# Edge convolution on Trainium2: three products by differences of rows for two blocks of rows, and norms in pairs of images

## The chip, the cores and the metric

The kernel runs on one core of one Trainium2 chip. The metric is the device time of one execution in microseconds (us). PE is the core's TensorE, DVE its VectorE, ACT its ScalarE, POOL its GpSimd; SP is the sync engine, which here only issues transfers. Everything is float32.

## The reference

The network works on 16 images of 32 channels and 128 x 128 pixels through four layers, each `x = x + layer(group_norm(x))`. The change touches the start of the last layer, which is cut here to what matters:

```python
def _norm(x):                     # over all channels and pixels of one image
    return (x - mean(x)) / std(x)

def get_operator(x):              # five edge maps, 3x3 taps, reflecting pad
    b1 = _norm(0.5*corr(x, SOBEL_X) + 0.5*corr(x, SOBEL_Y))
    b2 = _norm(0.5*corr(x, SCHARR_X) + 0.5*corr(x, SCHARR_Y))
    b3 = _norm(corr(x, LAPLACE3))
    b4 = _norm(0.5*corr(x, ROBERTS_X) + 0.5*corr(x, ROBERTS_Y))
    b5 = _norm(0.5*corr(x, PREWITT_X) + 0.5*corr(x, PREWITT_Y))
    return concatenate([b1, b2, b3, b4, b5], axis=1)      # 160 channels

y = maxpool2(conv3x3(get_operator(x), conv1_w, conv1_b))  # 160 -> 32 channels
# six more convolutions, two poolings and three deconvolutions follow,
# and the layer returns x * y
```

Edge operator and first convolution are linear, so the kernel joins them for each image into one 5 x 5 convolution of 32 to 32 channels, whose weights depend on the image through the five means and standard deviations.

## The kernel before

`network` (line 2072) runs layer0, layer1_offsets, layer1_scan, layer1_sample, layer2, layer3_edges and layer3_net one after the other. Only `layer3_edges` (line 1436) is concerned. It makes the joint convolution and the horizontal half of its pooling, and writes the result to `p1` in HBM; `layer3_net` takes the rest of the pooling and of the layer from there.

The input of an image lies in tile `t` (`image`, line 1708): 128 partitions are 4 image rows x 32 channels, and the free dimension has 33 such groups of four rows, each of 132 pixels. Group i of `t` holds the image rows 4i-2 to 4i+1. The four output rows 4r to 4r+3 therefore need groups r and r+1, and the weights stand in two matrices, `W[:, 0]` for group r and `W[:, 1]` for group r+1, for each of five horizontal taps. The next taps (5 to 10) of `W` hold weights for the corrections of the left and right border. `conv` (line 1788) makes four groups of output rows at once into one PSUM bank: 5 taps x 2 matrices, ten matmuls of 128 x 128 by 512 (line 1794). The first and last step of an image add matmuls for the upper and lower border (lines 1802 and 1807). VectorE adds the border columns' corrections in PSUM (line 1812) and takes the maximum of horizontal neighbours (line 1813). Every fourth step ScalarE's queue issues four transfers to `p1` (line 1859). An image has eight steps.

Before an image can be convolved its five means and variances must be known. `stats` (line 1560) is a generator: an image is two strips, and a strip loads tile `a`, makes the five edge maps on VectorE (lines 1586 to 1614), and ScalarE sums each map and its square in two passes (`keep`, lines 1577 to 1583, passes at 1579 and 1581). It yields six times in a strip. Maps live in five rotating buffers with the tag `f`; the row sums `R`, `H` (in R's buffer) and `B2` have a buffer each. `weights` (line 1630) turns the statistics of a batch of images, at most four, into `Eb`, `Bb` and `vec`: two small matmuls for means and variances, then twenty for the weights (lines 1668 and 1672) in PSUM tiles `pw` copied by ScalarE, and a last few (lines 1687 to 1701), with `rm` copied by VectorE (line 1691). `expand` (line 1733) spreads one image's part of that over the partitions by 14 transfers on SP's queue. `corrections` (line 1751) makes the border columns of an image by small matmuls (lines 1759 to 1779) and a ScalarE copy (line 1785).

The loop at line 1838 goes over the images. It loads the next image, makes the corrections of this one and its eight steps, and after each step advances the statistics generator by two (line 1853) if they are not far enough ahead. After the fifth step it makes the weights of the next batch, if the next image opens one. The batches are images 0; 1; 2 and 3; 4 and 5; 6 and 7; 8 to 11; 12 to 15 (`cut_at`, line 1822). PSUM has four banks for `ps`, two for the tag `pg` and one for `pc`.

The order of instructions inside an engine is not written out by hand in this function. The framework lays each engine's queue in advance, by the order of the program as a priority and a cost model's idea of when operands are ready; other layers fix the order with `in_order` (line 48), this one doesn't. [...]

Of the kernel before, what the change touches and what calls it, by code (L numbers as in the profile page):

```python
# [10 lines left out]
F32 = mybir.dt.float32  # L11
AF = mybir.ActivationFunctionType
ALU = mybir.AluOpType
AX = mybir.AxisListType
PSUM = bass.MemoryType.PSUM
DRAM = bass.MemoryType.DRAM

P = 128
B, T, HW = 16, 32, 128
# [1416 lines left out]
def layer3_edges(tc, w, x3, p1, sb3, b3, groups=range(NG)):  # L1436
# [4 lines left out]


    nc = tc.nc
    V = nc.vector
    NB = 11 * 5 * T
    NX = NB + 2 * 3 * 11 * T
    with ExitStack() as ctx:
        cp = ctx.enter_context(tc.tile_pool(name="ec", bufs=1))
        psum = ctx.enter_context(tc.tile_pool(name="ep", bufs=4, space=PSUM))
        psg = ctx.enter_context(tc.tile_pool(name="epg", bufs=2, space=PSUM))  # L1450
        psc = ctx.enter_context(tc.tile_pool(name="epc", bufs=1, space=PSUM))
        bcol = load(nc, cp, w["c1_b"], "c1_b")
# [3 lines left out]
        ones = cp.tile([P, P], F32, name="ones", tag="ones")  # L1456
# [103 lines left out]
        def stats(images, mv):  # L1560
# [4 lines left out]
            for n, (b, h) in enumerate(strips):  # L1565
# [7 lines left out]
                def made(tag, rows=16, cols=HW):  # L1573
                    bufs = 5 if tag == "f" else 1
                    return fp.tile([P, rows, cols], F32, name=tag, tag=tag, bufs=bufs)

# [31 lines left out]
                keep(4, f5)  # L1608
                H = made("R", 18, HW + 1)[:, :, 0:HW]
                V.tensor_add(H, a[:, :, 2 : HW + 2], a[:, :, 0:HW])  # L1610
# [140 lines left out]
        def corrections(j, t, W, Wb, vec):  # L1751

            e = slice(32 * j, 32 * j + 1)
            pc = psc.tile([P, 2, 32], F32, name="pc", tag="pc")
            first = True
# [31 lines left out]

        def conv(n, j, t, W, Wb, vec, cs, pl):

            ps = psum.tile([P, 4, HW], F32, name="ps", tag="ps")  # L1790
            low = 1 if n == 7 else 0
            for i in range(10):
                k, d = divmod(i, 5)
                nc.tensor.matmul(  # L1794
                    ps, W[:, k, d], t[:, 4 * n + k : 4 * n + k + 4, d : d + HW],
                    start=(i == 0), stop=(i == 9 and n not in (0, 7)), skip_group_check=True,
                )
            if n in (0, 7):
                e = slice(32 * j, 32 * j + 1)
                o = ps[96 * low : 96 * low + 32, 3 * low]  # L1800
                for d in range(5):
                    nc.tensor.matmul(
                        o, Wb[:, low, d], t[:, 32 * low, d : d + HW],
                        start=False, stop=False,
                        tile_position=(0, 96 * low), skip_group_check=True,
                    )
                nc.tensor.matmul(
                    o, vec[e, low], ones[e], start=False, stop=True,
                    tile_position=(32 * j, 96 * low), skip_group_check=True,
                )  # L1810
            v = ps[:, :, 0 : HW : HW - 1]
            V.tensor_add(v, v, cs[:, :, 4 * n : 4 * n + 4].rearrange("p s r -> p r s"))
            V.tensor_reduce(
                pl[:, 4 * (n % 4) : 4 * (n % 4) + 4],
                ps.rearrange("p y (x c) -> p y x c", c=2), AX.X, ALU.max,
            )

# [3 lines left out]
        made = 0  # L1821
        cut_at = [0, 1, 2, 4, 6, *range(8, len(images), 4), len(images)]

        def advance(upto):
            nonlocal made
            while made < upto:
                next(it, None)
                made += 1

        def batch(m):  # L1830

            end = min(c for c in cut_at if c > m)
            advance(12 * end + 1)
            return weights(images[m], images[end - 1] + 1, mv)

        vec = batch(0)
        nxt = image(*divmod(images[0], 4)), *expand(0)
        for m, b in enumerate(images):
            g, j = divmod(b, 4)
            t, W, Wb = nxt  # L1840
            v = vec
            if m + 1 < len(images):
                g1, j1 = divmod(images[m + 1], 4)
                t1 = image(g1, j1)
                if m + 1 not in cut_at:
                    nxt = t1, *expand(j1)
            cs = corrections(j, t, W, Wb, v)
            for n in range(8):
                if n % 4 == 0:
                    pl = op.tile([P, 16, 64], F32, name="pl", tag="pl")  # L1850
                conv(n, j, t, W, Wb, v, cs, pl)
                if m < 6 or made < 12 * (m + 2) + 3 * n:
                    advance(min(made + 2, 12 * len(images) + 1))
                if n == 4 and m + 1 < len(images) and m + 1 in cut_at:
                    vec = batch(m + 1)
                    nxt = t1, *expand(j1)
                if n % 4 == 3:
                    for r in range(4):
                        nc.scalar.dma_start(
                            p1[g][T * j : T * j + T, r, 4 * n - 12 : 4 * n + 4],  # L1860
                            pl[32 * r : 32 * r + 32],
                        )

# [451 lines left out]
```

## Time and profile before

| quantity | value |
| --- | --- |
| median of 3 runs | 17435.32 us (17428.0 to 17453.31) |
| the profiled execution's own time | 17403.99 us |
| its span, first to last instruction | 17402.1 us |
| mean granted clock of TensorE | 0.938 |
| busy over the span: PE, DVE, ACT, POOL | 89%, 84%, 70%, 56% |
| first strip of statistics of layer3_edges starts | 14887.3 us |
| last strip of statistics ends | about 16172.9 us |
| last pooling (line 1813) ends | about 16519.2 us |
| last transfer of pooled rows lands | about 16524.6 us |

The profile is of one execution. A window's row gives the busy time of each engine, the number of its instructions in brackets, then the clock granted to TensorE (1.0 is full speed), the busy share of the DMA engines and GB/s. A group's row gives the source line, the engine, the operation, output and inputs with their shapes and the count; after the first bar the busy time in us and the mean of one in ns; after the second the engine's idle time just before these instructions and what ended most of it. A row of waits gives who waited for whom, the total in us, how often, and the longest. A row of the chain gives start and length in us. Shares of busy time over the whole span are averages over seven layers; what bounds layer3_edges is read from its own stretch.

### The profile page before, as it was taken

The page shows a single profiled execution, that of the slowest core. Times are in us where ns is not written, and L with a number is a line of the kernel's source. Part 1 is how long each engine was busy: PE and PEld are TensorE (multiplying, and loading weights), DVE is VectorE, ACT ScalarE, POOL GpSimd, SP SyncE. Part 2 cuts the span into 40 slices and gives each one's busy share as a digit, 9 for nine tenths or more (in the row PEclk, how much of TensorE's full clock was granted, in tenths as well). Part 3 has the DMA queues.
Part 4 walks back from the last instruction along what each step waited for, and adds up shares of the span by engine and source line. Part 5 has one row for each costly group of instructions (what it writes and reads, how often), then busy time and mean ns, then how long its engine had stood idle before and what let it go on. Part 6 is the DMA issues. An engine that isn't in the chain of part 4 may idle for free. (4 is left out here: it accounts for less than half of the span.)

```text
span 17402.1 us, 300113 instructions
## 1 busy us (share of the span) xinstructions
PE 15532.7 (89%) x113588; PEld 5966.0 (34%) x113588; DVE 14616.2 (84%) x14651; ACT 12173.3 (70%) x23604; POOL 9783.9 (56%) x18465
## 2 busy tenths in 40 slices
PE   8999999999999888888888888899999988699988
PEld 3333333333333222222222222255555552244433
DVE  9999999999999769999999999888888886777223
ACT  7888888888888557777777777688888882565111
POOL 9999999999999527778887788500000000000000
PEclk9999999999999989999999999898999889788988
DMA  0000000000000574445544445577777779444245
GB/s 22 12 12 12 12 12 17 12 12 12 12 16 7 84 145 160 160 161 159 162 163 156 164 164 167 160 191 196 195 195 196 199 177 222 71 84 76 57 122 176
DMA packets 1519824, 1884.48 MB, mean 108 GB/s; under 512 B 146789, under 2 KB 866717, under 8 KB 1507558
## 3 DMA queue, kind: packets, MB, share of 16 engines
q1 hardware_dynamic: 1413414, 1688.04, 37.6%
q0 software_dynamic: 26624, 93.35, 1.6%
q10 hardware_dynamic: 78336, 83.90, 1.5%
q8 instruction: 893, 14.63, 0.3%
q14 instruction: 557, 4.56, 0.1%
HBM read 1561.58 MB, written 229.64 MB: 103 GB/s over the span
## 5 line engine op out<-in xcount | busy, mean ns | idle before, releaser
L235 POOL TENSOR_SCALAR Rp<-su,nv 128x128 f32<-128x128 f32 x16384 | 5804.7, 373 | 84.7 <-PE pS L241 50.9
L224 DVE TENSOR_TENSOR Rd<-pu,nv 128x2048 f32<-128x2048 f32 x2176 | 4881.3, 2279 | 69.5 <-PE pS L241 65.6
L239 ACT ACTIVATE Ra<-su,bv 128x128 f32<-128x128 f32 x14336 | 4284.7, 388 | 530.2 <-PE pS L241 523.0
L241 PE MATMUL pS<-Rd,zw 128*32 128x512 f32 x17408 | 2903.6, 603 | 221.4 <-DVE Rd L224 220.3
L822 DVE TENSOR_TENSOR_SCAN hh<-dd,state,pd 128x512 f32<-128x512 f32 x2304 | 2824.1, 1267 | 151.6 <-PE py L856 13.5
L843 POOL TENSOR_TENSOR hh<-hh,bc 128x2048 f32<-128x2048 f32 x512 | 2319.2, 4530 | 467.0 <-DVE state L830 455.5
L241 PE MATMUL pS<-Rp,zw 128*32 128x512 f32 x8192 | 1998.6, 597 | 164.1 <-POOL Rp L235 158.3
L807 PE MATMUL pd<-du,spread 32*128 32x512 f32 x4608 | 1349.5, 660 | 570.1 <-DVE hh L822 563.0
L1228 POOL DMA_DIRECT2D x<-ob x64 | 91.5, 1430 | 3107.3 <-DVE ob L1227 2770.4
L799 ACT ACTIVATE dd<-dd,m_a 128x512 f32<-128x512 f32 x2304 | 1515.4, 714 | 336.9 <-DMA dd<-dm 329.2
L817 DVE TENSOR_TENSOR pd<-pd,bc 128x1024 f32<-128x1024 f32 x1152 | 1401.5, 1217 | 57.3 <-ACT bc L780 56.6
L241 PE MATMUL pS<-Ra,zw 128*32 128x512 f32 x7168 | 1273.3, 599 | 0.0
L1236 ACT ACTIVATE yd<-yd,nrow 128x2048 f32<-128x2048 f32 x512 | 1238.2, 2418 | 46.4 <-DMA yd<-ymap 46.4
L1116 ACT ACTIVATE ya<-pb,nrow 128x1024 f32<-128x1024 f32 x1024 | 1191.3, 1250 | 85.3 <-PE pb L1115 85.2
L1115 PE MATMUL pb<-Y,sel 32*128 32x512 f32 (+1 forms) x5120 | 1080.7, 740 | 165.9 <-ACT ya L1116 163.1
L1794 PE MATMUL ps<-t,W 128*128 128x512 f32 x2560 | 1146.6, 607 | 0.0
L241 PEld LDWEIGHTS pS<-Rd,zw 128*32 128x32 f32 x17408 | 615.2, 109 | 1236.4 <-issue 593.2
L807 PEld LDWEIGHTS pd<-du,spread 32*128 32x128 f32 x4608 | 373.3, 191 | 1608.6 <-DVE hh L822 713.3
L1120 DVE TENSOR_SCALAR yd<-yd 128x2048 f32<-128x2048 f32 x512 | 726.5, 1419 | 197.1 <-ACT yd L1236 195.8
L241 PEld LDWEIGHTS pS<-Rp,zw 128*32 128x32 f32 x8192 | 440.5, 110 | 1303.0 <-POOL Rp L235 845.0
L1120 DVE TENSOR_SCALAR ya<-ya 128x2048 f32<-128x2048 f32 x512 | 760.1, 1484 | 11.1 <-ACT ya L1116 9.9
L1127 PE MATMUL pd<-ya,xt 128*32 128x128 f32 x16384 | 690.7, 311 | 41.9 <-DVE ds L1280 30.0
(411 smaller groups left out, 23131.6 us busy)
## 6 DMA issues: line engine op xcount, KB each, us to landing
dd<-dm SPq DMA_DIRECT2D x2304, 256.0 KB
yd<-ymap SPq DMA_DIRECT2D x512, 1024.0 KB
hw<-x SPq DMA_DIRECT2D x192, 512.0 KB
dm<-dt POOLq DMA_DIRECT2D x192, 256.0 KB, 3.7
xb<-tok SPq DMA_DIRECT2D x248, 144.0 KB
w<-d SPq DMA_DIRECT2D x64, 528.1 KB
x<-in_x SPq DMA_DIRECT2D x64, 512.0 KB
x<-o SPq DMA_DIRECT2D x128, 256.0 KB
```

What stands on the lines that cost most here:

```text
L224: nc.vector.tensor_tensor(R, st["pu"].unsqueeze(1).to_broadcast([P, 4, 4, HW]), nv[:, :, i::32].rearrange("p t q -> p q t").unsqueeze(3).t ...
L235: nc.gpsimd.tensor_scalar(R[:, q, k], su[:, k], 3.4028234e38, nv[:, k, c], ALU.min, ALU.max)
L239: nc.scalar.activation(R[:, q, k], su[:, k], AF.Relu, bias=bv[:, k, c])
L241: nc.tensor.matmul(st["pS"][32 * q : 32 * q + 32], zw[:, 31 - i : 63 - i], R[:, q], start=first, stop=False, tile_position=(0, 32 * q), sk ...
L799: S.activation(dd[:, r], dd[:, r], AF.Exp, scale=acol[:, dr, d : d + 1])
L807: nc.tensor.matmul(pd[:, a], spread[e, k], st["du"][n][e], start=True, stop=True)
L817: V.tensor_mul(pd, pd, bm.unsqueeze(1).to_broadcast([P, 2, CH]))
L822: V.tensor_tensor_scan(hh[:, r, s], dd[:, r, s], pd[:, a, s], st["state"][:, 4 * i + r : 4 * i + r + 1], ALU.mult, ALU.add,)
L843: G.tensor_mul(hh, hh, st["bc"][1, n].unsqueeze(1).to_broadcast([P, 4, CH]))
L1116: S.activation(dst[:, 2 * h : 2 * h + 2], pb, AF.Abs, bias=nrow)
L1120: V.tensor_scalar(t, t, 1.0, 1.0, ALU.min, ALU.subtract)
L1236: S.activation(yd, yd, AF.Abs, bias=nrow)
```

## The change

Two neighbouring groups of output rows, r and r+1 with r even, are

    y(r)   = W0 t(r)   + W1 t(r+1)
    y(r+1) = W0 t(r+1) + W1 t(r+2)

which is four products. The changed kernel makes three:

    both   = (W0 + W1) t(r+1)
    y(r)   = both + W0 (t(r)   - t(r+1))
    y(r+1) = both + W1 (t(r+2) - t(r+1))

A step of `conv` covers eight groups of rows, and an image has four steps. A new function `prepare` makes an image's corrections, the sum of the two matrices (into the taps 5 to 9 of `W[:, 0]`, which only the corrections read) and a copy of the last group of `t`; it is called after the third step of the image before, together with `expand`. A new function `differences` makes the differences on VectorE, one half into a tile `d` with one buffer, the other in place in `t`; it is called behind the last step of the image before. ScalarE copies the product `both` to SBUF, VectorE adds it to each of the two others into a tile `y`, and corrections and maximum work on `y`. The pooled rows leave after every step of eight groups. The batches of norms become images 0; 1; and then pairs. The statistics advance by four after a step, under a changed condition. Maps, `R`, `H` and `B2` share five buffers of one size. PSUM has five banks for `ps` and three for `pg`, which takes `pc` too.

```diff
-        psum = ctx.enter_context(tc.tile_pool(name="ep", bufs=4, space=PSUM))
-        psg = ctx.enter_context(tc.tile_pool(name="epg", bufs=2, space=PSUM))
-        psc = ctx.enter_context(tc.tile_pool(name="epc", bufs=1, space=PSUM))
+        psum = ctx.enter_context(tc.tile_pool(name="ep", bufs=5, space=PSUM))
+        psg = ctx.enter_context(tc.tile_pool(name="epg", bufs=3, space=PSUM))
...
                 def made(tag, rows=16, cols=HW):
-                    bufs = 5 if tag == "f" else 1
-                    return fp.tile([P, rows, cols], F32, name=tag, tag=tag, bufs=bufs)
+                    t = fp.tile([P, 18 * (HW + 1)], F32, name=tag, tag="f", bufs=5)
+                    return t[:, 0 : rows * cols].rearrange("p (r w) -> p r w", w=cols)
...
-                H = made("R", 18, HW + 1)[:, :, 0:HW]
+                H = made("H", 18)
...
-            pc = psc.tile([P, 2, 32], F32, name="pc", tag="pc")
+            pc = psg.tile([P, 2, 32], F32, name="pc", tag="pg")
...
+        def prepare(g, j, t, W, Wb, vec):
+
+            cs = corrections(j, t, W, Wb, vec)
+            V.tensor_add(W[:, 0, 5:10], W[:, 0, 0:5], W[:, 1, 0:5])
+            end = sp.tile([P, HW + 4], F32, name="end", tag="end")
+            nc.scalar.copy(end, t[:, 32])
+            return g, j, t, W, Wb, vec, cs, end
+
+        def differences(t):
+            d = xp.tile([P, 16, HW + 4], F32, name="d", tag="d", bufs=1)
+            V.tensor_sub(d, t[:, 0:32:2], t[:, 1:33:2])
+            V.tensor_sub(t[:, 2:33:2], t[:, 2:33:2], t[:, 1:33:2])
+            return d
...
+            def product(w, x, row=None):
+                ps = psum.tile([P, 4, HW], F32, name="ps", tag="ps")
+                for dx in range(5):
                     nc.tensor.matmul(
+                        ps, w[:, dx], x[:, :, dx : dx + HW], start=(dx == 0),
+                        stop=(dx == 4 and row is None), skip_group_check=True,
                     )
...
+            both = op.tile([P, 4, HW], F32, name="both", tag="both", bufs=2)
+            nc.scalar.copy(both, product(W[:, 0, 5:10], t[:, r + 1 : r + 8 : 2]))
+            pl = op.tile([P, 8, 64], F32, name="pl", tag="pl")
+            for k in range(2):
+                if k == 0:
+                    ps = product(W[:, 0, 0:5], d[:, 4 * n : 4 * n + 4], (0, 0, t[:, 0]) if n == 0 else None)
+                else:
+                    ps = product(W[:, 1, 0:5], t[:, r + 2 : r + 9 : 2], (1, 3, end) if n == 3 else None)
+                y = op.tile([P, 4, HW], F32, name="y", tag="y", bufs=1)
+                V.tensor_add(y, ps, both)
...
-        cut_at = [0, 1, 2, 4, 6, *range(8, len(images), 4), len(images)]
+        cut_at = [0, 1, *range(2, len(images) + 1, 2)]
...
+            for n in range(4):
+                conv(n, now, d)
+                if m < 3 or made < 12 * (m + 2) + 4 * n:
+                    advance(min(made + 4, 12 * len(images) + 1))
+                if n == 2 and more:
+                    if m + 1 in cut_at:
+                        vec = batch(m + 1)
+                    nxt = prepare(g1, j1, t1, *expand(j1), vec)
+            if more:
+                d = differences(t1)
```

More of the change, by code (lines that the diff above doesn't have):

```diff
@@ L1786, in corrections @@
             return cs
[L1788 to L1796, printed above, removed]
-                )
[L1798 to L1809, printed above, removed]
-                )
[L1811 to L1816, printed above, removed]
@@ new lines, in conv @@
+        def conv(n, now, d):
+            g, j, t, W, Wb, vec, cs, end = now
+            e = slice(32 * j, 32 * j + 1)
+            r = 8 * n
+            def product(w, x, row=None):
+                ps = psum.tile([P, 4, HW], F32, name="ps", tag="ps")
+                for dx in range(5):
+                    nc.tensor.matmul(
+                        ps, w[:, dx], x[:, :, dx : dx + HW], start=(dx == 0),
+                        stop=(dx == 4 and row is None), skip_group_check=True,
+                    )
+                if row is not None:
+                    low, m, x = row
+                    o = ps[96 * low : 96 * low + 32, m]
+                    for dx in range(5):
+                        nc.tensor.matmul(
+                            o, Wb[:, low, dx], x[:, dx : dx + HW], start=False, stop=False,
+                            tile_position=(0, 96 * low), skip_group_check=True,
+                        )
+                    nc.tensor.matmul(
+                        o, vec[e, low], ones[e], start=False, stop=True,
+                        tile_position=(32 * j, 96 * low), skip_group_check=True,
+                    )
+                return ps
+            both = op.tile([P, 4, HW], F32, name="both", tag="both", bufs=2)
[8 more added lines that the diff above has]
+                V.tensor_add(y, ps, both)
+                v = y[:, :, 0 : HW : HW - 1]
+                V.tensor_add(
+                    v, v, cs[:, :, r + k : r + k + 7 : 2].rearrange("p s r -> p r s")
+                )
+                V.tensor_reduce(
+                    pl[:, k:8:2], y.rearrange("p y (x c) -> p y x c", c=2), AX.X, ALU.max
+                )
+            for k in range(4):
+                nc.scalar.dma_start(
+                    p1[g][T * j : T * j + T, k, r : r + 8], pl[32 * k : 32 * k + 32]
+                )
@@ L1836, in layer3_edges @@
         vec = batch(0)
-        nxt = image(*divmod(images[0], 4)), *expand(0)
+        g, j = divmod(images[0], 4)
+        nxt = prepare(g, j, image(g, j), *expand(j), vec)
+        d = differences(nxt[2])
         for m, b in enumerate(images):
[L1839 to L1842, printed above, removed]
+            now = nxt
+            more = m + 1 < len(images)
+            if more:
                 g1, j1 = divmod(images[m + 1], 4)
                 t1 = image(g1, j1)
[L1845 to L1862, printed above, removed]
+            for n in range(4):
[6 more added lines that the diff above has]
+                    nxt = prepare(g1, j1, t1, *expand(j1), vec)
+            if more:
+                d = differences(t1)
 def layer3_net(tc, w, x3, p1, out, sb3, b3, groups=range(NG)):
```

## The prediction

> **What bounds the kernel now.** I read the cut of the span into windows first, then the groups of the edge convolution's time by line and form, its waits, and the chain that ended last. The change touches layer3_edges alone, which runs from 14887 us (first strip of statistics) to 16518.6 us (last pooling). The windows cut its image loop, roughly, into images 0 and 1, 2 and 3, 4 and 5, 6 and 7, 8 to 11, 12 to 15.
>
> ```profile
> core 0: us, PE busy (x) PEld busy (x) DVE busy (x) ACT busy (x) POOL busy (x), PEclk, DMA share, GB/s
> 15010.00:15262.00 252.00, 230.50 (x690) 97.17 (x689) 178.53 (x152) 142.78 (x191) 2.88 (x14) 0.87 0.40 70
> 15262.00:15453.00 191.00, 188.44 (x532) 81.00 (x531) 153.17 (x126) 121.27 (x160) 3.28 (x16) 0.89 0.47 83
> 15453.00:15651.00 198.00, 191.82 (x543) 83.07 (x539) 151.33 (x119) 119.39 (x155) 3.28 (x16) 0.88 0.42 75
> 15651.00:15887.00 236.00, 194.81 (x543) 87.10 (x544) 181.11 (x143) 148.16 (x190) 3.68 (x18) 0.83 0.46 84
> 15887.00:16222.00 335.00, 334.83 (x1049) 156.19 (x1048) 194.78 (x169) 145.09 (x187) 6.16 (x30) 0.98 0.35 66
> 16222.00:16519.00 297.00, 296.24 (x900) 138.25 (x898) 27.51 (x65) 13.88 (x13) 4.33 (x31) 0.98 0.23 47
> ```
>
> PE is never idle for long, but VectorE (DVE) follows at about 150 us in each 195. Only in the last row, where the statistics are over, is PE alone. So there are two parts: up to 16172 us (last strip done) two engines are near their limit, after it one is. The chain shows the pure PE part, and that the order inside an engine is not the program's (line 1603 stands after line 1598 in the program):
>
> ```profile
> 14899.05 2.20 DVE f L1603
> 14901.25 2.20 DVE f L1598
> ...
> 16299.69 60.43 PE ps L1794 x140
> ...
> 16377.98 60.43 PE ps L1794 x140
> ```
>
> 140 passes take 60.43 us, 0.432 us each. A float32 matmul is two passes in the trace (2560 = 16 images x 8 blocks x 10 taps x 2), so an image's convolution is 160 x 0.432 = 69.1 us; from one image to the next it is 78.3 us, the other 9.2 us being border rows and corrections. The groups give the prices:
>
> ```profile
> L1794 PE MATMUL ps<-t,W 128*128 128x512 f32 x2560 | 1146.6, 607 | 0.0
> ...
> L1579 ACT ACTIVATE f<-f 128x2048 f32<-128x2048 f32 x160 | 304.6, 1904 | 300.3 <-DVE f L1588 138.9 <-DVE f L1598 110.5 <-DVE f L1607 25.9
> L1813 DVE TENSOR_REDUCE pl<-ps 128x256 f32<-128x512 f32 x128 | 88.0, 688 | 2.3
> L1586 DVE TENSOR_TENSOR R<-a 128x2322 f32<-128x2322 f32 x32 | 82.3, 2571 | 13.5 <-DMA a<-x 12.2 <-ACT a L1557 1.1
> ...
> L1603 DVE TENSOR_TENSOR f<-a 128x2048 f32<-128x2048 f32 x32 | 73.1, 2285 | 0.1
> ```
>
> and the waits from 14887 to 16172 us show where VectorE's time goes unused:
>
> ```profile
> DVE ps L1812 <- PE ps L1794: 148.4, 37, 7.7
> ...
> DVE rm L1691 <- PE pr L1687: 68.0, 4, 22.9
> ...
> DVE ps L1812 <- PE ps L1807: 43.0, 12, 9.6
> ```
>
> In that stretch of 1285 us VectorE was busy 963.5 us (same windows view, one window), so unused 321.5: 191.4 waiting for convolution products (the first and third line), 94.8 waiting at line 1691 for the norm's matmuls (68.0, and 26.8 put down to line 1672), 35 in small gaps.
>
> [...] the batch of norms from 15208 to 15241 us, after gaps of 6.4, 6.7 and 7.5 us, was granted 0.50 and took 33 us; the one from 16178 to 16203 us, without a gap, 1.00 and 25 us with some convolution among it. [...] line 1691 stood up to 22.9 us with strip work behind it. [...]
>
> **Part by part.** Products: eight groups of rows now take three products of 5 taps, 30 passes or 12.96 us, where they took 40 passes, 17.3 us. Per image 120 passes, 51.8 us, instead of 69.1; with the unchanged 9.2 us an image is 61.0 us of PE, 17.3 less, 276 us over 16 images. That is an upper bound, as most of it lies beside VectorE's work.
>
> VectorE per image: 8 adds of product and copy, PSUM and SBUF to SBUF, 512 elements: lines 283 and 266 do that shape in 0.674 and 0.679[...]; 0.69 x 8 = 5.5. The small add (0.17) and the pooling (0.69) stay, now in SBUF. Two differences of 2112 elements: [...] between lines 1603 (2.285) and 1586 (2.571): 4.7. [...] Together 11.0 us an image. This lies on the engine with least room.
>
> ScalarE per image: 4 copies of 512 from PSUM (line 189: 0.572) 2.3; one row of 132, 0.25 (line 1725: 0.25 for 33 elements) to 0.30; 8 more DMA issues at 0.31 to 0.43 on its queue, 3.4 at most. 6 us an image: I take nothing, as ScalarE is 60% busy and the rest covers it; without cover 16 x 6 = 96. The pooled rows leave in two buffers for every eight groups instead of every sixteen; the last transfer took 5.34 us and a step takes 13 or more, so nothing, or the excess if it lands late. Its new wait is different: the copy waits for a PE product, with the statistics' Square and Identity passes queued behind it, and VectorE waits for those to get its map buffers back. From zero (PE is ahead) to one product, 4.3 us, four times an image.
>
> Buffers: the maps, R, B2 and H share five buffers where there were seven. A map is done on ScalarE about 4.4 us after VectorE made it and its buffer is wanted again five tiles, some 11 us, later. So nothing, unless ScalarE is over 6 us late; then each such case costs VectorE the excess. PSUM banks 4+2+1 become 5+3: between a small gain and nothing, I take nothing.
>
> Norms: nine batches for seven, each 25 (warm) to 33 us (cold) of PE and 2.84 us of VectorE, whose wait at line 1691 averaged 94.8/6 = 15.8. Against that, no batch needs four images' statistics at once: the 236 us window, with 25 us of empty PE, goes.
>
> Moves: expanding the weights (14 SP issues, 8 x 0.63 + 6 x 0.57 = 8.5 us, behind the strip loads; two POOL memsets of 0.4) and the corrections go from the image's start to the third of four steps of the image before. The fourth step's three products (13 us) hide them; uncovered, 8.5 us and a landing would stand before the image. The weights' sum waits for the corrections and the differences stand behind the image's last steps of statistics: new waits at each image's start. With the differences made, the first product that uses them is 4.3 us away, and the second another 4.3; VectorE needs about 1.6 us of work in between, so it waits some 5 us (0, if strip work is put there, to 17 if PE is cold and each takes 8.6).
>
> The sum, as VectorE's ledger to its last strip. Busy 963.5. Added, for 13.75 images instead of 12 pooled by then: adds 110 x 0.69 = 76; 14 more poolings at 0.86 = 12; differences 14 x 4.7 = 66; weights' sums 14 x 0.82 = 11; two batches 6: together 171. Unused: 8 batches x 15.8 = 126, 14 image starts x 5 = 70, small gaps 35: 231 instead of 321, since the waits for products, 191, came from a PE that filled the whole 191 to 198 us of a pair, and now needs 122 + 33 = 155. The last strip ends at 14887 + 964 + 171 + 231 = 16253. From there the last batch took 31 us before (16172.9 to 16204), corrections and sum 6, two images 122, last pooling 2: 16414 against 16518.6. Saved 105 us. The profiled execution took 17404.0 us with a span of 17402.1, so 17299 of it; the median of the three runs is 17435.3, 31 above, and with the same saving gives 17330.
>
> **Rivals.** (a) The ledger above: 17330. (b) VectorE finds strip work for most of its waits, which the free order of the queues allows, and only batches stop it: unused 130 instead of 231, saved 206, 17230. PE's own sum allows it: from 15016, 16 x 61 + 9 x 30 = 1246 to 16262, and about 50 of early waiting for statistics, as before at 15186 to 15208. (c) The unused time stays 321 because every engine now waits for another; saved 15, 17420. For it: ScalarE's new wait and the five buffers. Against it: PE has 35 us of slack in a pair. (d) Slower: at each image start VectorE stands for cold products. Mechanism: the differences stand behind up to four steps of statistics (about 18 us); PE has only the shared product to do[...]. It decides above 5 + 105/14 = 12.5 us per start; at 17, 14 x 12 = 168 more, 63 lost, 17498. For it: PEclk already 0.83 to 0.89 where both engines work. Against it: the free order can bring the differences forward.
>
> **Numbers.** Chances: (a) 0.47, (b) 0.20, (c) 0.16, (d) 0.17. A measurement of this kernel tells 0.2%, 35 us, from no change, so from 17400 to 17470 counts as none. (a) and (b) are faster, (c) mostly within, (d) slower: 0.70, 0.13, 0.17. The range takes (a) to (c) with the bounds of the costs, 25 to 30 us on each side: 17200 to 17450, leaving out (d).
>
> **What would show it.** PE's convolution passes at 1920 with the same 0.432 us when warm; a pure image 61 us at the end; 128 adds at 0.69 and 32 differences at 2.36; last strip near 16253, last pooling near 16414; pairs of some 176 us; VectorE over 85% busy between. Wrong if pairs exceed 187 us, the average before from 15242 us, when image 2 starts, to 16362, when image 14 does, or PEclk falls below 0.8 there.

## The result, and the profile after

The changed kernel takes 17368.33 us (median of 5 runs, 17350.89 to 17383.67) beside 17443.89 us for the kernel before (5 runs, 17428.0 to 17481.99): a ratio of 0.9952, 95% interval 0.9938 to 0.9967, or 76 us saved where 105 were forecast. The profiled execution took 17350.89 us, its span is 17349.1 us, the mean granted clock 0.931. The first strip of statistics starts at 14891.0 us (before 14887.3), the last ends at 16271.8 us (forecast 16253), the last pooling at 16460.5 us (forecast 16414, before 16519.2).

In the lines of the changed kernel the products are at 1812, the copy `both` at 1831, its add at 1839, the pooling at 1844, the differences at 1799 and 1800, the sum of the matrices at 1792, the norms' matmuls at 1648, 1654, 1669, 1673 and 1688, and the copy `rm` at 1692. The windows cut the image loop, roughly, into pairs of images (us, then busy time and count of PE, PEld, DVE, ACT and POOL, then granted clock, DMA share, GB/s):

```profile
15025.00:15269.00 244.00, 182.42 (x513) 76.66 (x514) 189.33 (x163) 134.62 (x184) 3.39 (x16) 0.76 0.36 65
15269.00:15428.00 159.00, 148.91 (x463) 68.09 (x464) 145.60 (x131) 99.92 (x137) 2.99 (x14) 0.90 0.51 91
15428.00:15620.00 192.00, 164.82 (x463) 71.76 (x464) 138.69 (x127) 99.50 (x136) 3.39 (x16) 0.78 0.41 73
15620.00:15809.00 189.00, 160.92 (x479) 70.08 (x478) 158.00 (x136) 112.40 (x151) 3.39 (x16) 0.80 0.48 86
15809.00:15994.00 185.00, 161.16 (x447) 70.36 (x448) 137.77 (x127) 95.48 (x129) 3.39 (x16) 0.80 0.42 75
15994.00:16178.00 184.00, 162.58 (x494) 71.21 (x493) 145.87 (x130) 103.49 (x143) 3.39 (x16) 0.81 0.45 83
16178.00:16341.00 163.00, 159.19 (x465) 69.63 (x466) 98.16 (x110) 72.41 (x99) 3.39 (x16) 0.86 0.31 58
16341.00:16460.00 119.00, 117.80 (x346) 54.52 (x345) 31.82 (x53) 9.44 (x13) 1.49 (x19) 0.96 0.16 35
```

The last row is two images of PE alone, 119 us, at a granted clock of 0.96: the saving is there in full. From the first pooling of image 14 to the last pooling the kernel before took 141 us (16378 to 16519), the changed one 106 (16354 to 16460): 35 less, and two images at 17.3 are 34.6. All 14 images ahead of them, which have 14 x 17.3 = 242 us fewer of products, are only 24 us earlier (28 counted from the first strip). Only images 2 and 3, the row from 15269, still keep both engines over 90% busy. In the four rows from 15428 to 16178, VectorE is busy 138 to 158 us of 184 to 192, and PE, which has 122 us of images to do there at full clock, shows 161 to 165 at a granted clock of 0.78 to 0.81.

Where the rest went can be counted in the two timelines of PE: the stretches of more than 8 us in which no product runs, from the first product on, are six before, of 9 to 81 us, and add up to 243 us; in the changed kernel they are eight, of 20 to 94 us, and add up to 463. These 220 us more are about what is missing.

The timeline of PE around the end of one pair shows what such a stretch holds (start, us, engine, line and operation, in brackets PE's idle time before it and what ended it):

```profile
15546.26 4.47 PE L1812 MATMUL ps<-t,W 128*128 128x512 f32 x10
15550.66 1.28 PE L1820 MATMUL ps<-end,Wb 128*32 128x128 f32 x10
...
15557.42 0.60 PE L1648 MATMUL pm<-ms,avg 128*128 128x10 f32 x2 [5.14 <-DVE ms L1644]
15563.55 0.60 PE L1654 MATMUL pv<-ms,avg 128*128 128x10 f32 x2 [5.54 <-DVE ms L1652]
15569.20 1.86 PE L1669 MATMUL pw<-base,l 128*64 128x480 f32 x2 [5.04 <-DVE l L1664]
...
15607.37 1.46 PE L1760 MATMUL pc<-t,W 128*128 128x32 f32 x6 [4.13 <-DMA W<-Eb]
...
15619.58 2.08 PE L1812 MATMUL ps<-t,W 128*128 128x512 f32 x2 [6.92 <-DMA a<-x]
```

The batch of norms for the next two images lies behind the last product of this pair, so PE has nothing else to do. It waits three times some 5 us for VectorE, the twenty `pw` matmuls run at half clock (0.50 granted) until 15598.9, then come the transfers of the expanded weights, the corrections and the weights' sum (the profile puts the last wait down to a load of `a`; the sum ended at 15619.52, so it was the sum). From 15552.3, the last border matmul, to 15619.6 no product runs: 67 us. Two images at 61 and that gap are 189. The batches for images 2, 8, 10 and 12 stand behind the last product in the same way, in gaps of 65 to 94 us. Only the one for images 4 and 5 began among products; its `pw` matmuls ran at full clock (1.00 granted, 1.02 us a pair), in a gap of 35 us.

VectorE shows the other side of the same gap. Its waits until the last strip (who waited for whom, total us, times, longest):

```profile
DVE rm L1692 <- PE pr L1688: 106.0, 6, 25.8
DVE y L1839 <- PE ps L1812: 48.8, 16, 7.0
DVE rm L1692 <- PE pw L1673: 26.8, 2, 13.9
DVE y L1839 <- PE ps L1824: 19.7, 9, 3.3
```

and its timeline in the gap:

```profile
15557.43 2.28 DVE L1595 TENSOR_TENSOR f<-B 128x2048 f32<-128x2048 f32 x1
...
15559.72 0.15 DVE L1649 COPY mean<-pm 128x10 f32<-128x10 f32 x1
...
15560.47 2.28 DVE L1598 TENSOR_TENSOR f<-a 128x2048 f32<-128x2048 f32 x1
...
15599.43 0.21 DVE L1692 COPY rm<-pr 5x64 f32<-5x64 f32 x1 [25.76 <-PE pr L1688]
15599.57 2.54 DVE L1611 TENSOR_TENSOR H<-a 128x2304 f32<-128x2304 f32 x1
...
15618.70 0.82 DVE L1792 TENSOR_TENSOR W<-W 128x640 f32<-128x640 f32 x1
```

The small steps of the norm stand between map operations of 2.28 us, so each answer to PE takes some 5 us; then VectorE stands for 25.8 us at `rm`, with map work queued behind it; and the sum of the two matrices, at 15618.70, stands behind eight map operations made since `rm`, while PE, done with the corrections at 15612.65, waits for it. Each engine waits for the other in turn.

The groups give the prices that the prediction used:

```profile
L1812 PE MATMUL ps<-t,W 128*128 128x512 f32 x1280 | 610.4, 628 | 60.1 <-DVE W L1792 53.2 <-DMA a<-x 6.9
L1812 PE MATMUL ps<-d,W 128*128 128x512 f32 x640 | 291.8, 601 | 0.0
L1839 DVE TENSOR_TENSOR y<-ps,both 128x512 f32<-128x512 f32 x128 | 87.8, 686 | 169.5 <-PE ps L1812 115.8 <-PE ps L1824 43.6 <-ACT f L1580 6.5
L1799 DVE TENSOR_TENSOR d<-t 128x2112 f32<-128x2112 f32 x16 | 37.6, 2352 | 23.4 <-PE ps L1812 20.0 <-issue 3.4
L1792 DVE TENSOR_TENSOR W<-W 128x640 f32<-128x640 f32 x16 | 13.1, 820 | 10.1 <-PE pc L1760 10.0 <-DMA a<-x 0.2
L1831 ACT COPY both<-ps 128x512 f32<-128x512 f32 x64 | 37.3, 582 | 235.7 <-PE ps L1812 210.1 <-DMA p<-pl 14.1 <-issue 8.1
```

1920 passes, adds of 0.686, differences of 2.35, a sum of 0.82 and copies of 0.58 us are what was priced.

### The profile page after: what moved, and what is told of

It is laid out like the page before. It is cut to its first block, busy times and chain, and to the rows that moved or that the text cites. A ratio compares the mean times of both kernels' runs of the same rounds, so it can differ in the third digit from the quotient of the medians.

```text
span 17349.1 us, 299637 instructions
## 1 busy us (share of the span) xinstructions
PE 15374.5 (89%) x113040; PEld 5889.8 (34%) x113040; DVE 14782.1 (85%) x14857; ACT 12219.8 (70%) x23708; POOL 9818.0 (57%) x18465
## 5 line engine op out<-in xcount | busy, mean ns | idle before, releaser
L1127 PEld LDWEIGHTS pd<-yd,xt 128*32 128x32 f32 x16384 | 539.8, 178 | 470.2 <-issue 232.9
```

What stands on the lines that cost most here:

```text
L1127: M(pd[32 * q : 32 * q + 32, i], xt[:, :, xc], h, start=True, stop=True, tile_position=(0, 32 * q),)
```

## The experiments

The theories. **A** is the prediction's: VectorE's ledger, its work and its waits one after the other, sets when the last strip ends, and PE is beside it. **B**, the serial theory: a pair of images costs PE two images and, behind them, a batch of norms at half clock with nothing beside it; VectorE has room. **C** was formed after the first four runs: B holds with three products only, since with four the batch falls among convolutions; for the run relief it adds that the strips come too late, so that with less work for VectorE the batch would fall among them again. The expectations of the last runs call B so limited the serial theory.

Each ratio is to the kernel before, run beside it on the same chip; the medians of before were 17443.89 us beside the changed kernel, 17422.75 beside the next four rows, 17413.43 beside the four after them and 17406.84 beside the last four, so rows of different groups are compared by their ratios. The profiled positions count from the start of the span. The layers ahead of the stage took up to 89 us more in one profiled execution than in another, so positions of two kernels are compared from the first strip; the last column is the time from there to the last pooling, of one execution each (before: 14887.3, 16172.9, 16519.2, and 1631.9).

| kernel | median us (runs) | ratio to before, 95% interval | first strip starts, last strip ends, last pooling ends (profiled) | first strip to last pooling |
| --- | --- | --- | --- | --- |
| changed kernel | 17368.33 (5) | 0.9952, 0.9938 to 0.9967 | 14891.0, 16271.8, 16460.5 | 1569.5 |
| four_products | 17353.78 (10) | 0.9962, 0.9946 to 0.9977 | 14869.2, 16240.2, 16443.4 | 1574.2 |
| after_quads | 17425.91 (14) | 0.9998, 0.9987 to 1.001 | 14857.6, 16202.8, 16502.9 | 1645.3 |
| before_pairs | 17402.04 (22) | 0.999, 0.9981 to 0.9999 | 14883.9, 16288.9, 16500.9 | 1617.0 |
| own_sum | 17363.81 (18) | 0.9966, 0.9955 to 0.9977 | 14886.6, 16272.7, 16466.0 | 1579.4 |
| early | 17285.19 (4) | 0.9927, 0.9899 to 0.9955 | 14925.5, 16227.7, 16437.8 | 1512.3 |
| rm_first | 17329.37 (9) | 0.995, 0.9935 to 0.9964 | 14883.7, 16256.1, 16447.4 | 1563.7 |
| relief | 17319.57 (7) | 0.9943, 0.9924 to 0.9962 | 14898.3, 16254.1, 16448.8 | 1550.5 |
| four_late | 17360.65 (20) | 0.9969, 0.9959 to 0.9979 | 14943.2, 16323.3, 16531.0 | 1587.8 |
| early_relief | 17229.15 (4) | 0.9898, 0.9883 to 0.9913 | 14886.4, 16125.4, 16340.4 | 1454.0 |
| four_early | 17327.81 (5) | 0.9955, 0.9942 to 0.9969 | 14859.6, 16167.3, 16451.4 | 1591.8 |
| four_psum | 17337.4 (5) | 0.9958, 0.9943 to 0.9973 | 14903.2, 16275.9, 16479.3 | 1576.1 |
| all3 | 17254.13 (6) | 0.9913, 0.9897 to 0.993 | 14854.7, 16143.0, 16350.9 | 1496.2 |

**The products alone, undone: four_products.** The changed kernel's frame (pairs, preparation one image ahead, steps of eight groups, buffers and banks), with four products in PSUM and neither differences, sum, copy nor adds.

```diff
-            both = op.tile([P, 4, HW], F32, name="both", tag="both", bufs=2)
-            nc.scalar.copy(both, product(W[:, 0, 5:10], t[:, r + 1 : r + 8 : 2]))
...
+                for i in range(10):
+                    q, dx = divmod(i, 5)
+                    nc.tensor.matmul(
+                        ps, W[:, q, dx], t[:, r + k + q : r + k + q + 7 : 2, dx : dx + HW],
...
-                V.tensor_add(y, ps, both)
```

> The changed kernel with the old four products in its new frame (pairs of norms, prepare, steps of eight groups, shared buffers); the differences, the weights' sum, the copy and the 128 adds are left out. Theory A (VectorE's ledger sets the end of the statistics): VectorE has 11 us less an image, PE 17.3 more, and PE becomes the limit as before, with pairs of about 195 us, so 17440 to 17480 us. Theory B (a pair is two images of PE and then, one after the other, a batch of norms during which PE has nothing else): a pair becomes 157 + 50 to 62 = 207 to 219 us, seven of them, so 17530 to 17610.

Measured: 17353.78 us, 0.9962, within the interval of the changed kernel. Both theories forecast a slower kernel and missed, A by 86 us and B by 176. The three products by themselves gained nothing that can be measured; the frame gained what there is. Windows of three pairs of four_products:

```profile
15250.00:15425.00 175.00, 175.00 (x542) 78.74 (x540) 153.79 (x127) 117.75 (x156) 3.38 (x16) 0.99 0.41 79
15425.00:15600.00 175.00, 174.60 (x541) 79.07 (x540) 96.06 (x89) 79.55 (x107) 3.38 (x16) 0.98 0.40 77
15600.00:15777.00 177.00, 177.00 (x547) 79.45 (x546) 126.36 (x108) 94.11 (x126) 3.39 (x16) 0.99 0.43 81
```

PE is hardly ever idle (0.4 us in these 527) and has nearly its full clock, 0.98 to 0.99, for the batch lies among convolutions, in PE's timeline of the same kernel:

```profile
15373.88 0.29 PE L1648 MATMUL pm<-ms,avg 128*128 128x10 f32 x2
15374.02 7.99 PE L1809 MATMUL ps<-t,W 128*128 128x512 f32 x18
15381.85 0.28 PE L1654 MATMUL pv<-ms,avg 128*128 128x10 f32 x2
15381.99 4.55 PE L1809 MATMUL ps<-t,W 128*128 128x512 f32 x10
15386.46 1.02 PE L1669 MATMUL pw<-base,l 128*64 128x480 f32 x2
```

A `pw` pair takes 1.02 us here and 1.86 in the changed kernel. Without the convolution among them, its matmuls take 18 us of PE. So a pair with four products is 2 x 78.3 + 18 = 175 us, and one with three 2 x 61 + 67 = 189: the gap gives back more than the products save. This was the ground for C. It is the frame with four products that hides its batches; in the kernel before itself most of them stood in gaps too (57, 36, 42 and 81 us at images 2, 4, 6 and 8).

**The batches: after_quads and before_pairs.** The one list of batches, exchanged in each kernel.

```diff
-        cut_at = [0, 1, *range(2, len(images) + 1, 2)]
+        cut_at = [0, 1, 2, 4, 6, *range(8, len(images), 4), len(images)]
```

> The changed kernel with the old batches of norms (0; 1; 2-3; 4-5; 6-7; 8-11; 12-15). A: VectorE's ledger is two batches' waits (2 x 16 us) and the pooling of two images (34 us) shorter, but four images of 61 us stand behind the last batch instead of two, +122: 17400 to 17430. B: two serial batches of 62 us less, some 60 us of starving for four images' statistics more: 17290 to 17330.

> The kernel before with the pairs as batches and nothing else. A and B agree that each of two more batches costs PE 34 to 50 us and that the stretch of starving before images 8 to 11 (25 us) goes: 17480 to 17520. If the pairs by themselves were a gain it would be below 17420.

Measured: with batches of four the changed kernel is as slow as the kernel before, 0.9998; pairs alone in the kernel before give 0.999, some 20 us. So pairs are worth 0.46%, 80 us, to the changed kernel, and little to the other. For after_quads A's range held (17425.91 in 17400 to 17430) and B's failed. A's two terms came out smaller, though: from the first strip, the last strip is 36 us earlier than in the changed kernel, where A's sum of waits and pooling was 66, and 111 us more stand behind it, where A had 122. For before_pairs both theories forecast a slower kernel, 17480 to 17520, and missed. PE's waits for the statistics from 14830 to 16520 us are 347.4 us in after_quads and 153.1 in the changed kernel, in this order:

```profile
PE pm L1648 <- DVE ms L1644: 347.4, 6, 121.9
```

```profile
PE pm L1648 <- DVE ms L1644: 153.1, 6, 101.9
```

A PE that gets through its images sooner stands the longer for a batch that needs four more images' strips.

**VectorE's work: relief.** Two of the twelve map operations of each strip go.

```diff
-                E1 = made("f")
-                V.tensor_sub(E1, a[:, 0:16, 2 : HW + 2], a[:, 2:18, 0:HW])
...
-                V.tensor_add(f5, f5, E1)
```

> The changed kernel with two of the twelve VectorE operations of a strip left out (the term E1 of the fifth map, so the fifth norm is of another map), 64 x 2.2 = 141 us less VectorE work. A: 17220 to 17260. B: pairs stay at 122 + 62 = 184: 17340 to 17370. C: strips are done while PE still convolves, so the batch is hidden as with four products, and the gain is nearly as large as with A or larger, pairs of 150: 17150 to 17240, with PE's clock up from 0.79.

Measured: 17319.57 us, 0.9943, within the changed kernel's interval; from the first strip, the last strip ends only 25 us earlier. The stage's window of each kernel, the changed one first, from 14900 to 16270 us:

```profile
14900.00:16270.00 1370.00, 1110.71 (x3214) 482.85 (x3215) 1103.57 (x953) 793.16 (x1070) 22.43 (x106) 0.79 0.42 75
```

```profile
14900.00:16270.00 1370.00, 1140.86 (x3243) 494.64 (x3244) 981.72 (x904) 799.97 (x1083) 22.77 (x108) 0.79 0.42 76
```

In this window VectorE's busy time falls by 122 us and its unused time rises from 266 to 388. Counted in each kernel from its own first strip to its last, busy time falls by 137 (1114.3 to 977.0) and unused time rises by 112 (266.5 to 378.8): VectorE spends the time waiting, for products alone 121 us instead of 69. A ledger would have passed the work on; A falls. C's addition falls too. B's range, 17340 to 17370, is the nearest, missed by 20 us. The batch is still behind the last product (PE's timeline of relief):

```profile
15537.85 0.40 PE L1821 MATMUL ps<-ones,vec 1*32 1x128 f32 x2
15543.13 0.60 PE L1645 MATMUL pm<-ms,avg 128*128 128x10 f32 x2 [4.88 <-DVE ms L1641]
15549.27 0.60 PE L1651 MATMUL pv<-ms,avg 128*128 128x10 f32 x2 [5.54 <-DVE ms L1649]
15554.92 1.86 PE L1666 MATMUL pw<-base,l 128*64 128x480 f32 x2 [5.04 <-DVE l L1661]
```

The program ties the strips to the steps of convolution: at image m, step n, it goes no further than 12 (m+2) + 4n and four more, which after the third step is just what the batch called there asks for. Less work for VectorE doesn't bring the batch forward. But the pacing isn't the whole reason: four_products has it too, and there the batch stands in its place in the program, behind the third step. Why the order laid in advance puts the fourth step's products ahead of the batch with three products was not found out.

**The waits inside the gap: own_sum and rm_first.** The first gives the sum of the matrices a tile of its own, so that it needn't wait for the corrections; the second issues `pr`, `rm`, `pvec` and `pb` ahead of the loop of `pw` matmuls.

```diff
+            Ws = wp.tile([P, 5, 4 * T], F32, name="Ws", tag="Ws")
+            V.tensor_add(Ws, W[:, 0, 0:5], W[:, 1, 0:5])
             cs = corrections(j, t, W, Wb, vec)
-            V.tensor_add(W[:, 0, 5:10], W[:, 0, 0:5], W[:, 1, 0:5])
```

> The changed kernel with the sum of the two weight matrices in a tile of its own, made before the corrections instead of over the taps that they read, so that it waits for no correction. PE stood 53 us for that sum, seven times. B: these lie on the serial chain of a pair, so about 50 us go: 17310 to 17330. A: VectorE's ledger stays, only the last one (about 9 us) is past it: 17350 to 17370.

> The changed kernel with the small matmuls and VectorE's copy of rm put ahead of the twenty weight matmuls of a batch instead of behind them, so that VectorE doesn't stand for them (133 us in all up to the last strip). A: VectorE gets some 100 us back: 17250 to 17290. B and C: strips are earlier, but a pair is still two images and a batch alone, gain at most what PE idles before the batches (51 us): 17320 to 17370.

Measured: 17363.81 and 17329.37 us, 0.9966 and 0.995; neither differs from the changed kernel. For own_sum A's range held and B's failed, for rm_first the range of B and C held and A's failed. In the profile of own_sum PE waits 63.8 us for the sum instead of 53.2:

```profile
PE ps L1813 <- DVE Ws L1792: 63.8, 7, 11.4
```

It isn't the corrections that held the sum up, but its place in VectorE's queue: at the same pair it stands again behind eight map operations made since `rm`. In rm_first the waits for `rm` are gone from VectorE's list, but 112 us of waits for map buffers that ScalarE still reads have taken their place, half of them in this row:

```profile
DVE f L1595 <- ACT f L1582: 56.1, 5, 21.3
```

In the longest of these, ScalarE is held from 15569.8 to 15599.5 by its ten copies of `pw`, each behind a pair of matmuls (29.7 us in all, as at the 0.50 granted in the changed kernel), with its passes over the maps queued behind them; VectorE fills the free buffers until 15583.9 and then stands for 21.3 us. So the batch holds VectorE through ScalarE as well: what one wait gave back, another took.

**The batch's place: early.** Each pair's norms are made one image earlier (in the first image of the pair before, after its third step), with the statistics allowed one image further ahead.

```diff
-                if m < 3 or made < 12 * (m + 2) + 4 * n:
+                if m < 3 or made < 12 * (m + 3) + 4 * n:
...
-                    if m + 1 in cut_at:
+                    if m < 2:
                         vec = batch(m + 1)
+                    elif m % 2:
+                        vec = ahead
                     nxt = prepare(g1, j1, t1, *expand(j1), vec)
+                    if m > 1 and m % 2 == 0 and m + 2 < len(images):
+                        ahead = batch(m + 2)
```

> The changed kernel with each pair's norms made one image earlier: after the third step of the first image of the pair before, and the statistics kept an image further ahead. Nothing else. Theory C (formed after the first four runs: with three products PE has no convolution left when a batch starts, falls to half clock and carries the batch alone, about 62 us a pair, where with four products it hides it in 18): the batch now lies beside convolutions, pairs fall from 184 towards 160 to 165 and three images instead of two stand behind the last strip: 17260 to 17310. Theory A (VectorE's ledger alone): its waits at the batches are the same and one image more (61 us) stands behind the last strip: 17370 to 17430.

Measured: 17285.19 us, 0.9927, the fastest until then (its interval still meets the changed kernel's). C's range held, A's failed. PE's timeline of early at such a place:

```profile
15724.31 0.60 PE L1648 MATMUL pm<-ms,avg 128*128 128x10 f32 x2 [9.94 <-DVE ms L1644]
15728.35 0.60 PE L1654 MATMUL pv<-ms,avg 128*128 128x10 f32 x2 [3.44 <-DVE ms L1652]
...
15737.07 6.73 PE L1812 MATMUL ps<-t,W 128*128 128x512 f32 x8
15743.73 1.02 PE L1669 MATMUL pw<-base,l 128*64 128x480 f32 x2
...
15759.88 1.99 PE L1812 MATMUL ps<-d,W 128*128 128x512 f32 x4
```

The next image's weights were there already, so products stand on both sides of the `pw` matmuls, these take 1.02 us instead of 1.86, and all twenty 16 us (15743.7 to 15759.6) instead of 30. It isn't so everywhere: of the six batches for images 4 to 15, two still ran their `pw` matmuls in 29.7 us, as at the changed kernel's 0.50, from 15414.4 and from 16078.2. Counted between the first poolings, the four pairs of images 4 to 11 take 159, 162, 175 and 182 us, where the changed kernel's take 197, 184, 185 and 182; images 2 and 3 take longer (195 for 156), 12 and 13 less (139 for 162). The edit moves two things, the batch and the statistics that it needs; statistics further ahead with the batch left in its place were not tried.

**With the batch moved: early_relief, four_early, all3.** They are early with relief's edit, four_products with early's edit, and early with both edits of own_sum and rm_first.

> Leaves out the E1 term of the fifth edge map, as relief does (two of twelve VectorE operations of each strip, 141 us in all), in the kernel that makes each pair's norms one image earlier. Serial theory: the batch alone on PE was what kept VectorE's relief from showing; once it lies beside convolutions, PE needs 122 + some 25 a pair against pairs of 162 to 182, VectorE is the next limit, and taking its work away shows: some 80 us under early's 17285, about 17205. Rival (what limits early is still the chain of the batches, not VectorE's work): not more than the 49 us that relief gave without the move, about 17236 or above.

> Four products as before, in the frame of the changed kernel, with each pair's norms one image earlier. Serial theory: with four products PE was busy in all but 52 us of the stage at a clock near 1.0 and hid its batches already, so the move gives nothing: 17340 to 17365. Then the three products are worth some 65 us, but only with the batch moved. Rival (moving statistics and norms forward is good in itself, whatever the products): 60 us or more less, at or under 17295, and the three products are worth nothing even then.

> Three edits together on the changed kernel: norms of a pair one image earlier, the rm matmuls ahead of the twenty pw matmuls, the sum of the two matrices in a tile of its own. Serial theory: the first takes away most of what the second gained, since the batch is hidden already; rm first still spares VectorE part of its 113 us of waits at line 1692 that early has left, so 10 to 25 us under early, 17260 to 17275. If the gains add up (39 for rm first, 5 for the sum): about 17240. If they don't matter once the batch is early: 17285.

Measured: early_relief 0.9898, 0.0029 or 50 us under early; the expected size was 80, and the rival's 49 was the difference of two medians from different groups of runs, of which the ratios leave 16 (0.9952 to 0.9943). By ratios, then, VectorE's relief is worth 16 us with the batch in the open and 50 with the batch moved, and from the first strip to the last pooling 19 and 58; this speaks for the serial theory, but the intervals of the ratios meet in both cases, so neither size is shown. Some 141 us of work left out bring about a third of themselves, so VectorE isn't the one limit there either. What holds early up is not settled.

Four_early: 0.9955 beside 0.9962, nothing that can be measured, as the serial theory expected (its median, 17327.81, lies 12 us under the range given): PE idled 0.0 us from 15250 to 16250, and moving norms and statistics forward is no good in itself. Three products with the norms moved (early, 0.9927) are then 0.28% or 49 us better than four, and 80 us from the first strip to the last pooling, but the intervals of the ratios meet. Beside each other in one group of runs, all3 is 74 us faster than four_early, with intervals apart (0.9897 to 0.993 and 0.9942 to 0.9969). All3 has two smaller edits more, and four products with the `rm` matmuls first were not tried, so how much of the 74 us the three products make is not shown.

Of the kernels with all edge maps, all3 is the only one whose interval lies clear of the changed kernel's, and the fastest by median, 153 us under the kernel before; early and all3 can't be told apart by their ratios, so what the two smaller edits add on top is open.

**What the frame gained: four_late and four_psum.** Four_products with the corrections back at the start of their own image, and with PSUM in four, two and one banks.

```diff
-            now = nxt
+            now = prepare(*nxt)
...
-                    nxt = prepare(g1, j1, t1, *expand(j1), vec)
+                    nxt = g1, j1, t1, *expand(j1), vec
```

> The kernel with four products in the new frame, with the corrections and the copy of the last group made at the start of the image itself instead of after the third step of the image before. If the early corrections are what makes the frame faster than the kernel before: 17400 to 17440. If it is the pairs, the PSUM banks and the pacing: 17345 to 17370.

> Four products in the frame of the changed kernel, with PSUM cut as before (four banks for ps, two for pg, one for pc in place of five and three). If the banks are what the frame gains beyond the pairs of images (17402 for pairs alone in the kernel before, 17354 for the frame with four products), the time goes back to about 17400. If it is the preparation one image ahead, or the larger steps, it stays within 15 us of 17354, which I expect.

Measured: 17360.65 and 17337.4 us, 0.9969 and 0.9958, both within the interval of four_products, as expected to a few us. Neither the preparation one image ahead nor the banks alone make the 0.28% between before_pairs and four_products. What does, the steps of eight groups with statistics in fours, the five shared map buffers or the sum of small parts, wasn't tried.

## Why the prediction was right in its result, and where its steps failed

The time forecast, 17330, is 38 us under the measured one and within its range; faster by more than 0.2% was right. The way there was only partly right.

- **Prices and counts held.** Products 1920; an image of PE alone 61.1 us, from the first pooling of image 14 to that of image 15 (16354.0 to 16415.1), against 61.0; adds 0.686 against 0.69 (0.674 and 0.679 for that shape in before); differences 2.35 against 2.36 (between the 2.285 us for 2048 elements and the 2.571 for 2322 in before, a straight line gives 2.35); sum 0.82 (such a line from 0.679 for 512 to 2.285 for 2048 gives 0.81). That the shared product has to be copied before it is added was not shown: no run has the three products without the copy. That the 276 us of products are an upper bound held too: two images gave all of it, fourteen gave 24 of 242.
- **The ledger's terms held.** VectorE was busy 1114.3 us up to the last strip (forecast 963.5 + 171 = 1134.5) and unused 266.5 (forecast 231): line 1692 took 132.8 against 126, waits for products 68.5 against 70. The last strip came at 16271.8 against 16253.
- **The ledger as the cause failed.** Its step, that the waits for products "came from a PE that filled the whole 191 to 198 us of a pair, and now needs 122 + 33 = 155", made PE's time cover and left VectorE as the one that sets the end. Relief took 137 us out of VectorE's side and 25 came through. At the last pair it wasn't the strips that the images waited for at all: when the last strip ended, at 16271.8, PE still had products of image 13 to do, until 16293.4, and went on to the batch's first matmul without a wait. The ledger came out near the truth because its waits were estimated near what they became, and not because it bounds the stage: that was luck.
- **The term mis-sized is the batch.** I priced it at 25 to 33 us of PE and 31 + 6 at the end. The matmuls from `pw` to `pb` do take 32.6 at a granted 0.50, but before them lie three waits of 15.7 us in all, and behind them the expanded weights, the corrections and the sum, so the gap without a product is 67 us in the pair shown and 44 at the last batch, where no map work is left, instead of 37. The step that said "The fourth step's three products (13 us) hide them" is the one that failed: in six of the seven batches from image 2 on, the fourth step's products stood ahead of the batch in PE's queue, not behind it, and nothing hid the preparation of the next image. I named the price of lost cover for the expansion, 8.5 us and a landing, but not for the whole chain. At the end, the 46 us between 16414 and 16460.5 are 19 us of a later last strip (4 of them because the stage began later), 22 of products left over from image 13, 7 of the larger gap, and 1 less for the last two images (123 for 124).
- **Pairs.** From image 2 to image 14 they average 178 us (1066/6), forecast some 176, and before 186 (1114/6). But this mean hides two kinds: 156 and 162 us at the ends and 197, 184, 185, 182 between. The 237 us pair of before, with its wait for four images' statistics, is gone, as forecast.
- **Clock and shares.** Of my signs of error neither occurred: between images 2 and 14 the pairs stayed under 187 us in the mean and PEclk was 0.82, not below 0.8 (before 0.91). So the signs did not catch the wrong step. Only VectorE's share did: 76% in that stretch and 81% from the first strip to the last, not over 85%.
- **The half clock.** Here, behind gaps of 5.1, 5.5 and 5.0 us, the first `pw` pair took 1.86 instead of 1.02 us, as it did in before behind 6.4, 6.7 and 7.5. PE's own work didn't bring the clock back at once: the twenty `pw` matmuls ran without a gap for 29.7 us and stayed at 0.50, in before (from 15208) as here. It came back with the products behind the batch, to 1.00 from 15249 in before and from 15628 here. I used the 33 us of before for the batch's own price and not for what the product cut does to it: with less convolution, there was none left beside the batch in six of the seven from image 2 on, and these six began with a `pw` pair of 1.86 us.
- **Rivals.** (b), 17230, wanted PE's own sum to decide; it took the batch at 30 us too. (c) had the right mechanism, engines waiting for each other in turn, but its unused time, 321, was too large (266.5 measured); the 76 us saved lie between its 15 and the ledger's 105. In (d) cold products at image starts were to come from late differences: lines 1799 and 1800 waited 33 us in all; it was the sum and the batch that kept PE, in 7 image starts out of 16, and not VectorE standing for cold products. ScalarE's new wait occurred (210 us over 45 copies, 4.7 each, near the 4.3 that I named) and cost nothing that shows: map buffers kept VectorE waiting only a few us here. That ScalarE's room covers the rest was too simple all the same: in rm_first the batch held it, and VectorE waited 112 us for buffers.

## What to carry to other kernels

When a cut makes one engine's work shorter, look for what that work was hiding: here, in the same frame, four products kept PE busy at a granted 0.98 to 0.99 with the norms' batch among them (1.02 us for its first `pw` pair), and three left it in the open at 0.50 (1.86 us). Price a dependent chain by what stands on both sides of it in the queue, its hops through a busy engine (5.5 and 5.0 us at the pair shown, 1.8 and 1.3 at the last batch) and its followers included, not by the sum of its own instructions. Then give the chain a place where independent work exists, and test a supposed bound by taking work from it: if its unused time grows by nearly as much, it isn't one. One forecast that comes true is less of a test: after_quads met the range of the theory that relief refuted.

## What the runs showed of the hardware

At the pair shown, the two hops from PE through VectorE and back took 5.5 and 5.0 us, for VectorE steps of 0.15 to 0.2 us, because operations of 2.28 us ran between them. At the last batch, with no map work left, PE waited 1.8 and 1.3 us, and its first `pw` pair took 1.86 us all the same: there the clock was 1.00 until 16298.5 and 0.50 from the first `pw` matmul on, behind these two waits with only small matmuls between.

The twenty `pw` matmuls ran in 15.9 us at full clock (1.00) or in 29.7 us at half (0.50), and from image 2 on, in no batch of the changed kernel that began them at half clock did they bring it back, though they ran without a gap: all of the 30 us from 15569 have a granted clock of 0.50. Then products started again at 15619.6, and the clock is 0.50 until 15624 and 1.00 from 15628. In early, 15 us without a gap (15728.8 to 15743.7) that ended with eight passes of products in a row stood ahead of `pw` pairs of 1.02 us, after gaps of 9.9 and 3.4 us; at another batch of the same run 12 us (16066.3 to 16078.2), with six passes among corrections, stood ahead of the `pw` matmuls that took 29.7 us. What decides between the two, the runs don't show.
